# A message-passing layer on one core: the third update layer in an iteration of its own, first tables made on other engines, and a shorter order for the last blocks

## The chip, the core and the metric

The kernel runs on one core of a Trainium2 chip. Its time is the device time of one execution in microseconds. Engines are TensorE (PE, with its weight loads PEld), VectorE (DVE), ScalarE (ACT), GpSimd (POOL) and SyncE (SP, which issues DMAs). They run each their own list of instructions in order and wait for each other on semaphores.

## The reference

128 graphs of 64 nodes with 128 features. For each edge (i, j) of a graph a three-layer network (layer norm after the first two) gives a message; the messages of a node are summed, and a second such network updates the node:

```python
messages = _mlp(concat[f_i, f_j], msg_w0 ... msg_b2)
messages = messages * coupling_matrix[..., None]
agg = jnp.sum(messages, axis=2)
updated = part_feats + _mlp(concat[part_feats, agg], upd_w0 ... upd_b2)

def _mlp(x, w0, b0, g0, be0, w1, b1, g1, be1, w2, b2):
    h = _layernorm(jax.nn.relu(x @ w0 + b0), g0, be0)
    h = _layernorm(jax.nn.relu(h @ w1 + b1), g1, be1)
    return h @ w2 + b2
```

Some one in eight pairs has an edge, so the kernel computes messages only for listed edges.

## The kernel before, in words

**Edges.** Two graphs form a pair; each graph has 640 edge slots in 5 tiles of 128. A *chunk* is 4 tiles, a *quarter* 5 chunks (two pairs), a *block* 4 pairs (10 chunks). There are 160 chunks, 32 quarters and 16 blocks.

**The loop.** `edge_path` writes the program out as numbered iterations `n`. In each, PE does layer 1 of chunk n-8 (`layer1`, L546, bank `z`), layer 0 of chunk n (`layer0`, L499, bank `hps`), transposes `h` of chunk n-1 (`stats0`, L510, bank `hT`) and makes the selection marks of chunk n+2 (`marks`, L486, bank `mk`). DVE takes the statistics of `hT` (L518), compares `mk` with the table `cmpt` into `s` (L497) and takes the statistics of `y` (L564). ACT turns `hps` into `h` (L508) and `z` into `y` (L557). Beside this, each iteration has places ("a", "m", "b", "x", "x1", "x2", "e1", "e", run in the order at L905 to L922) to which a dictionary `plan` assigns functions by iteration number through `at(n, place, ...)`. An engine's order of work is the order in which this loop issues. So what stands at "a" goes first on ACT, what stands at "m" first on DVE, and what stands at "x" last on PE.

**Quarters.** `var0_of`, `root_of`, `turn_root` make the standard deviation of layer 0 (`m_sd`, `sh`, `sdT`), `var1_step`, `root1_of`, `inverse_of` the inverse one of layer 1 (`m_v`, `m_sq`, `m_q`). `node_marks` and `weights` (L625) make per-node weights `w`, and `reduce` (L637) sums messages per node into bank `ys`.

**The update of a block** is a `Unit`, a chain over 14 iterations: `sums_out` (`ysum`), a transpose (`turn`, `turn_out`), first layer from `xn` and `ysum` (`u0a`, `w2u`) with `layer_out` into `uh`, its statistics and root, a transpose, second layer (`u1c`) into `uy`, statistics and root, a transpose, third layer (`u2c`), and `finish` (L734), which writes `uo` and sends it out. `bias0` (L672) makes the additive part `m0` of the first layer, `residual` the one of the last. The last block is cut into two units of half its width.

**Banks.** All three layers of a unit, `rows` (the first-layer products of a block's nodes, L443) and the products of derived weights share the one bank `mu` (`ubank`, L316, one buffer); transposes share two banks `ma`.

**The start.** Constants and derived matrices are made while the first blocks run: `derivation` (L175) lists 13 products through `mu`, one per iteration, with scaled weights and broadcasts made on POOL (L181, L207) and the banks emptied by DVE (L190, L201). `bias_table` and `bias_part` (L569, L595) make the table `b1t` that layer 1 needs, the latter on ACT in 20 operations.

Of the kernel before, what the change touches and what calls it, by code (L numbers as in the profile page):

```python
# [23 lines left out]
def tile_gnn(  # L24
# [79 lines left out]
    def load_first(b, q0, q1):  # L104
# [37 lines left out]
    nc.vector.memset(lt, 1.0)  # L142
    nc.gpsimd.affine_select(out=lt, in_=lt, pattern=[[1, P]], compare_op=ALU.is_ge,
                            fill=0.0, base=0, channel_multiplier=-1)
    first = const.tile([P, PB, N], F32, name="first")
# [3 lines left out]
    make_identity(nc, ident)  # L149

# [11 lines left out]
    nc.vector.memset(lt[0:N, N:P], 0.0)  # L162

    slot = const.tile([P, CAP], F16, name="slot")
    nc.gpsimd.iota(slot, pattern=[[1, CAP]], base=0, channel_multiplier=0,
                   allow_small_or_imprecise_dtypes=True)
    cmpt = const.tile([P, 4 * CAP], F16, name="cmpt")
    nc.vector.memset(cmpt[0:N, 0:CAP], 1.0)
# [123 lines left out]
    def edge_path(es):  # L292
# [23 lines left out]
        def ubank():  # L316

            return ps_u.tile([P, 512], F32, name="mu")

# [275 lines left out]
        def bias_part(c):  # L595
            for t in range(CH * c, CH * c + CH):
                nc.scalar.activation(W["b1t"][:, t, :], W["b1mix"], AF.Copy,
                                     scale=W["tile_of"][:, t:t + 1])
# [26 lines left out]
        def weights(p):  # L625
# [3 lines left out]
            for g in range(2):  # L629
                k = (2 * h + g) * TG  # L630
                (nc.vector if p == NP - 2 else nc.gpsimd).tensor_tensor(  # L631
# [21 lines left out]
        class Unit:  # L653


            def __init__(self, b, k0, n, eng):
                self.b, self.k0, self.n, self.eng = b, k0, n, eng
                self.s = slice(k0 * P, (k0 + n) * P)
                self.q = slice(k0, k0 + n)
                self.blk = blocks[b]  # L660

        def wide(name, u):
            t = updp.tile([P, PB, C], F32, name=name)
            return t[:, 0:u.n, :]
# [24 lines left out]
        def turn_out(u, src):  # L689
            t = updp.tile([P, PB * P], F32, name=src + "T")  # L690
            setattr(u, src + "T", t)
            nc.scalar.copy(t[:, 0:u.n * P], u.ps[:, 0:u.n * P])

        def layer(u, *pairs):
            ps = ubank()
# [9 lines left out]
        def layer_out(u, o, bias):  # L705
# [3 lines left out]
            st = updp.tile([P, PB, 6], F32, name=o + "_st")[:, 0:u.n, :]  # L709
# [4 lines left out]
        def upd_m0(u):  # L714
            u.m2 = square_sum(updp, u.st, u.n, f"um0_{u.n}", u.eng)

        def upd_root0(u):
            u.sd = root0(updp, u.m2, u.n, f"um0_{u.n}")
# [6 lines left out]
        def upd_m1(u):  # L725
            u.v1 = var1_of(updp, u.st, u.m2, u.n, f"um1_{u.n}", u.eng)

        def upd_root1(u):
            u.v1 = root1(updp, u.v1, u.n, f"um1_{u.n}")

        def upd_inverse(u):
            u.q1 = inverse(updp, u.v1, u.n, f"um1_{u.n}")
# [15 lines left out]
        SC = QC + L1 + QC  # L748
        for b in range(NB):
# [23 lines left out]
            if b < NB - 1:  # L773
                units = [(Unit(b, 0, PB, nc.gpsimd), o + QC + SC)]
# [3 lines left out]
            for u, n in units:  # L778
                at(n + 1, "a", sums_out, u)
                at(n + 1, "e", bias0, u)  # L780
                at(n + 2, "x", turn, u, "ysum")
                at(n + 3, "a", turn_out, u, "ysum")
                at(n + 3, "x", lambda u: layer(u, ("xn", u0a), ("ysumT", W["w2u"])), u)
                at(n + 4, "m", layer_out, u, "uh", "m0")
                at(n + 4, "e", upd_m0, u)
                at(n + 6, "a", upd_root0, u)
                at(n + 6, "e", upd_shift, u)
                at(n + 7, "x", turn, u, "uh")
                at(n + 8, "a", turn_out, u, "uh")
                at(n + 8, "x", lambda u: layer(u, ("uhT", W["u1c"])), u)  # L790
                at(n + 8, "e", residual, u)
                at(n + 9, "m", layer_out, u, "uy", "usdb")
                at(n + 9, "e", upd_m1, u)
                at(n + 11, "a", upd_root1, u)
                at(n + 11, "m", upd_inverse, u)
                at(n + 12, "x", turn, u, "uy")
                at(n + 13, "a", turn_out, u, "uy")
                at(n + 13, "x", lambda u: layer(u, ("uyT", W["u2c"])), u)
                at(n + 14, "m", finish, u)
        for p in range(NP):  # L800
# [4 lines left out]
            at(w, "x", node_marks, p)  # L805
            at(w + 1, "a", node_marks_out, p)
            at(w + 2, "e1", weights, p)
            at(p // 2 * QC + SC, "x1", reduce, p)
# [280 lines left out]
```

## Time and profile before

| | us |
|---|---|
| median of 3 runs (lowest, highest) | 700.18 (699.29, 700.63) |
| profiled execution, its time | 698.02 |
| profiled execution, span from first to last instruction | 696.3 |
| PE busy | 636.4 (91%) |
| DVE busy | 503.2 (72%) |
| ACT busy | 359.0 (52%) |
| POOL busy | 361.8 (52%) |
| mean granted TensorE clock | 0.961 |

In the profile's rows, "L701 PE MATMUL mu<-u0a,xnT" is an instruction of line 701 on PE that reads `u0a` and `xnT` and writes `mu`; a bracket behind a row is the engine's idle time before it and what ended that. An fp32 matmul has two records. A busy share of PE is not its share of peak. PEclk is the granted clock, 1.00 being full.

### The profile page before, as it was taken

The numbers are of one execution on the slowest core, as the hardware profiler recorded it, in microseconds if no ns is written. First come the engines' busy times: TensorE is split into PE (matmuls) and PEld (weight loads), VectorE is DVE, ScalarE is ACT, GpSimd is POOL, SyncE is SP. The second block draws the span as 40 slices with busy tenths as digits, with TensorE's granted clock in tenths as the row PEclk, the third lists the DMA queues.
The fourth block names the chain that finished last, engine by engine and source line by source line (L and its number), as shares of the span: only waits on it lengthen the run. The fifth ranks groups of instructions, "written<-read, shape, count | busy, mean of one in ns | idle before, by whom it ended". The sixth has DMA issues, their size and how long they took to land.

```text
span 696.3 us, 15879 instructions
## 1 busy us (share of the span) xinstructions
PE 636.4 (91%) x5873; PEld 584.2 (84%) x5873; DVE 503.2 (72%) x1917; ACT 359.0 (52%) x814; POOL 361.8 (52%) x932
## 2 busy tenths in 40 slices
PE   6799999899998989989898998989899898989874
PEld 5688899798898979889897998989799898978762
DVE  6788778778587867858786785877768586776453
ACT  3655565555454546536454663645556364554330
POOL 7443555548274554827455382745638364453550
PEclk8999999999999999999999999999999999999986
DMA  5000000100101010010101001010000000000001
GB/s 130 16 24 1 9 2 1 40 2 1 39 2 39 2 39 1 2 39 1 39 2 39 2 1 39 3 39 2 7 25 2 16 2 16 1 2 16 16 2 32
DMA packets 27916, 12.06 MB, mean 17 GB/s; under 512 B 10422, under 2 KB 27836, under 8 KB 27836
## 3 DMA queue, kind: packets, MB, share of 16 engines
q1 hardware_dynamic: 27548, 10.89, 5.8%
q8 instruction: 47, 0.77, 0.5%
q14 instruction: 33, 0.27, 0.1%
q10 hardware_dynamic: 288, 0.13, 0.1%
HBM read 6.82 MB, written 4.19 MB: 16 GB/s over the span
## 4 chain that ended last, share of the span: by engine, by line


## 5 line engine op out<-in xcount | busy, mean ns | idle before, releaser
L518 DVE BATCH_NORM_STATS2 st<-hT 128x6 f32<-128x128 f32 x640 | 141.8, 283 | 69.6 <-PE hT L514 64.1
L554 PEld LDWEIGHTS z<-w1c,h 128*128 128x128 f32 x1280 | 168.4, 192 | 7.1
L554 PE MATMUL z<-w1c,h 128*128 128x128 f32 x1280 | 168.8, 274 | 0.0
L631 POOL TENSOR_TENSOR w<-oh,m_q 128x320 f32<-128x320 f16 x126 | 88.8, 726 | 114.2 <-PE hT L514 100.4
L564 DVE BATCH_NORM_STATS2 st<-y 128x6 f32<-128x128 f32 x640 | 137.5, 275 | 7.2 <-ACT y L557 7.2
L557 ACT ACTIVATE y<-z 128x512 f32<-128x512 f32 x160 | 95.9, 599 | 89.5 <-PE z L554 87.4
L508 ACT ACTIVATE h<-hps,b0c 128x512 f32<-128x512 f32 x160 | 109.3, 683 | 5.2 <-PE hps L505 5.2
L497 DVE TENSOR_TENSOR s<-mk,cmpt 128x512 fp32r<-128x512 f32 x160 | 107.4, 671 | 0.1
L514 PE MATMUL hT<-ident,h 128*128 128x128 f32 x640 | 97.4, 275 | 0.0
L505 PE MATMUL hps<-s,abl 128*128 128x512 f32 (+3 forms) x256 | 92.1, 371 | 2.8 <-ACT h L508 2.8
L514 PEld LDWEIGHTS hT<-ident,h 128*128 128x128 f32 x640 | 76.5, 141 | 9.7
L551 PE MATMUL z<-b1t,sdT 80*128 80x512 f32 x160 | 78.8, 492 | 1.1 <-ACT y L557 1.1
L505 PE MATMUL hps<-s,abh 128*128 128x512 f32 (+3 forms) x256 | 78.3, 324 | 0.0
L646 PE MATMUL ys<-y,w 128*64 128x128 f32 x1280 | 77.8, 277 | 0.0
L646 PEld LDWEIGHTS ys<-y,w 128*64 128x64 f32 x1280 | 70.1, 138 | 3.4 <-issue 0.2
L701 PE MATMUL mu<-u0a,xnT 128*128 128x128 f32 x128 | 34.8, 365 | 34.1 <-DVE uo L737 32.6
L490 PE MATMUL mk<-tp,qs 128*128 128x512 f16 (+3 forms) x256 | 61.4, 301 | 3.4 <-DVE s L497 2.8
L701 PEld LDWEIGHTS mu<-u0a,xnT 128*128 128x128 f32 x128 | 26.9, 259 | 37.3 <-DVE uo L737 35.3
L465 DVE TENSOR_TENSOR abl<-mu,abh 128x512 fp32r<-128x512 f32 x32 | 22.1, 690 | 49.0 <-ACT abh L458 49.0
L505 PEld LDWEIGHTS hps<-s,abl 128*128 128x128 f32 x256 | 49.5, 193 | 3.5 <-ACT h L508 3.2
L252 POOL TENSOR_TENSOR um_d<-uh_st 128x4 f32<-128x4 f32 x15 | 3.1, 207 | 92.6 <-DVE uh_st L711 92.6
L622 ACT CAST oh<-ma 128x384 f16<-128x384 f32 (+1 forms) x128 | 48.5, 433 | 3.5 <-PE ma L615 0.5
(209 smaller groups left out, 1104.5 us busy)
## 6 DMA issues: line engine op xcount, KB each, us to landing
xn<-in_x_dram SPq DMA_DIRECT2D x15, 256.0 KB, 3.2
out_dram<-uo SPq DMA_DIRECT2D x15, 256.0 KB, 2.4
an<-in_adj_dram SPq DMA_DIRECT2D x16, 128.0 KB, 3.0
xn<-in_x_dram SPq DMA_DIRECT2D x2, 128.0 KB
out_dram<-uo SPq DMA_DIRECT2D x2, 128.0 KB, 2.1
w<-in_L_gnn_msg_w_dram SPq DMA_DIRECT2D x2, 64.0 KB, 2.9
u<-in_L_gnn_upd_w_dram SPq DMA_DIRECT2D x2, 64.0 KB, 2.0
w0a<-in_L_gnn_msg_w_dram ACTq DMA_DIRECT2D x1, 64.0 KB, 2.1
```

The lines of the kernel that those rows point to most:

```text
L497: nc.vector.tensor_tensor(S[n], MK.pop(n), cmpt[:, o:o + CH * P], op=ALU.is_equal)
L505: nc.tensor.matmul(ps[:, c:c + w], lhsT=ab[:, g % 4, :], rhs=s[:, c:c + w], start=(k == 0), stop=(k == 1))
L508: nc.scalar.activation(H[n], ps, AF.Relu, bias=b0c)
L514: nc.tensor.transpose(ps[:, t, :], H[n][:, t * P:(t + 1) * P], ident)
L518: nc.vector.bn_stats(ST0[q][:, CH * c + t, :], ps[:, t, :])
L551: nc.tensor.matmul(ps, lhsT=SD[q], rhs=W["b1t"][:, CH * c:CH * c + CH, :], start=True, stop=False, skip_group_check=True)
L554: nc.tensor.matmul(ps[:, t, :], lhsT=h[:, t * P:(t + 1) * P], rhs=W["w1c"], start=False, stop=True, skip_group_check=True)
L557: nc.scalar.activation(Y[n], ps, AF.Relu)
L564: nc.vector.bn_stats(ST1[q][:, CH * c + t, :], Y[n][:, t, :])
L631: (nc.vector if p == NP - 2 else nc.gpsimd).tensor_tensor(w[:, :, g, :], OH[p][:, :, g, :], Q[q][:, k:k + TG].unsqueeze(2).to_broadcast([P ...
L646: nc.tensor.matmul(YS[b][g * N:(g + 1) * N, k, :], lhsT=w[:, t, g, :], rhs=y, start=(t == 0), stop=(t == TG - 1))
L701: nc.tensor.matmul(ps[:, s], lhsT=l, rhs=w, start=(n == 0), stop=(n == len(pairs) - 1))
```

## The change

Five parts:

1. *Order of a unit.* The fixed offsets become lists. In `STEADY` the third layer moves from offset 13 to 14 and `finish` from 14 to 15; before, offset 13 of one block and offset 3 of the next were the same iteration, and both use `mu`. `bias0` moves from offset 1 to -2.
2. *Last blocks.* `LAST` gives block 14 and the two half units of block 15 shorter lists; the second half unit starts 3 iterations earlier. The half units use the banks of `hps` and `z` (`hbank`, `zbank`), whose own work is over by then. The last quarter's marks are made two iterations earlier, its weights all on DVE, its root one iteration earlier. The first half unit's small statistics go from DVE to POOL.
3. *Tables at the start.* The constant memsets and `iota`s for `lt`, `cmpt`, `slot` and one element of `dq` go to POOL or ahead; `cmpt`'s second memset (1920 columns on DVE between two compares) becomes 960 columns on DVE at the very start and 1600 on POOL. The step table of block 0 comes from two matmuls into two banks, emptied by ACT and DVE at once.
4. *Derived matrices.* Scalings and broadcasts go from POOL to ACT, right ahead of their product; plain products are emptied by ACT instead of DVE. `bias_part` goes from ACT (4 operations a chunk) to POOL (one a chunk).
5. *Buffers.* A unit's tiles are one per block and shared by its half units; `uo` and the statistics have two buffers.

The core of the diff:

```diff
-            nc.gpsimd.tensor_scalar(wg, w, g, None, op0=ALU.mult)
             def product():
+                nc.scalar.activation(wg, w, AF.Copy, scale=g)
...
-                nc.vector.tensor_copy(W[name], ps[:, :C])
+                nc.scalar.copy(W[name], ps[:, :C])
...
-            nc.gpsimd.tensor_copy(beb, be.to_broadcast([P, P]))
             def fn(ps):
+                nc.scalar.copy(beb, be.to_broadcast([P, P]))
...
+        def hbank():
+            return ps_h.tile([P, CH * P], F32, name="hps")
+        def zbank():
+            return ps_z.tile([P, CH, C], F32, name="z").rearrange("p t c -> p (t c)")
...
         def bias_part(c):
-            for t in range(CH * c, CH * c + CH):
-                nc.scalar.activation(W["b1t"][:, t, :], W["b1mix"], AF.Copy,
-                                     scale=W["tile_of"][:, t:t + 1])
+            t = slice(CH * c, CH * c + CH)
+            nc.gpsimd.tensor_tensor(W["b1t"][:, t, :],
+                                    W["b1mix"].unsqueeze(1).to_broadcast([4 * QT, CH, C]),
+                                    W["tile_of"][:, t].unsqueeze(2).to_broadcast([4 * QT, CH, C]),
+                                    op=ALU.mult)
...
-                (nc.vector if p == NP - 2 else nc.gpsimd).tensor_tensor(
+                (nc.vector if p // 2 == NQ - 1 else nc.gpsimd).tensor_tensor(
...
         def layer(u, *pairs):
-            ps = ubank()
+            ps = u.bank()
...
+        STEADY = (1, 2, 3, 3, 4, 7, 8, 6, 8, 9, 12, 13, 11, 14, 15)
+        LAST = ((1, 2, 3, 3, 4, 4, 5, 6, 5, 7, 7, 8, 9, 8, 9),
+                (1, 1, 2, 2, 3, 3, 4, 4, 4, 5, 5, 6, 7, 6, 7),
+                (1, 2, 3, 3, 4, 4, 5, 5, 5, 6, 6, 7, 7, 7, 8))
...
-                units = [(Unit(b, 0, 2, nc.vector), o + SC), (Unit(b, 2, 2, nc.vector),
-                                                              o + QC + SC)]
+                units = [(Unit(b, 0, 2, nc.gpsimd, hbank), o + SC, LAST[1]),
+                         (Unit(b, 2, 2, nc.vector, zbank), o + QC + SC - 3, LAST[2])]
...
-                at(n + 1, "e", bias0, u)
+                at(n - 2, "e", bias0, u)
...
-                at(n + 13, "a", turn_out, u, "uy")
-                at(n + 13, "x", lambda u: layer(u, ("uyT", W["u2c"])), u)
-                at(n + 14, "m", finish, u)
+                at(n + t[11], "a", turn_out, u, "uy")
+                at(n + t[12], "a", upd_root1, u)
+                at(n + t[12], "m", upd_inverse, u)
+                at(n + t[13], "x", lambda u: layer(u, ("uyT", W["u2c"])), u)
+                at(n + t[14], "m", finish, u)
...
+            last = p // 2 == NQ - 1
+            m = w - 2 if last else w
+            at(m, "x", node_marks, p)
+            at(m + 1, "a", node_marks_out, p)
+            at(NCHK + L1 + 1 if last else w + 2, "e1", weights, p)
+            at(NCHK + L1 + 2 if last else p // 2 * QC + SC, "x1", reduce, p)
...
+        nc.gpsimd.memset(cmpt[0:N, 3 * CAP // 2:4 * CAP], 1.0)
...
+        for g in range(2):
+            ps = (abank, zbank)[g]()
+            nc.tensor.matmul(ps[:, 0:PB * N], lhsT=dq,
+                             rhs=blocks[0]["pos"].rearrange("p q j -> p (q j)"), start=True,
+                             stop=True)
...
-        nc.vector.memset(cmpt[0:N, CAP:4 * CAP], 1.0)
...
         for c in range(QC):
-            at(4 + c, "a", bias_part, c)
+            at(4 + c, "e", bias_part, c)
```

How the rows of the engines' lists move is shown at three places. First PE in the steady part, from the marks of the iteration in which a block's first update layer runs. Before (`u2c` is the third layer of the block ahead, `u0a` and `w2u` the first layer of this one):

```order
L490 MATMUL mk<-tp,qs 128x128
L701 MATMUL mu<-u2c,uyT 128x128 x4
L701 MATMUL mu<-u0a,xnT 128x128
L701 MATMUL mu<-w2u,ysumT 128x128
...
L421 MATMUL ma<-pos,dq 128x256
L538 MATMUL ma<-ident,sh 80x128
L551 MATMUL z<-b1t,sdT 128x512
L554 MATMUL z<-w1c,h 128x128 x4
```

and now, with the iteration behind it:

```order
L498 MATMUL mk<-tp,qs 128x128
L715 MATMUL mu<-u0a,xnT 128x128
L715 MATMUL mu<-w2u,ysumT 128x128
...
L429 MATMUL ma<-pos,dq 128x256
L546 MATMUL ma<-ident,sh 80x128
L559 MATMUL z<-b1t,sdT 128x512
L562 MATMUL z<-w1c,h 128x128 x4
...
L498 MATMUL mk<-tp,qs 128x512
L715 MATMUL mu<-u2c,uyT 128x128 x4
L443 MATMUL ma<-ident,xn 128x128 x4
```

`u2c` has moved from the place right ahead of `u0a` to the end of the next iteration.

Second POOL in the steady part, at the two operations of `bias0` (`c2u,deg` and `ub0b`). Before they stand behind the last operation of `var1_step` (`m_v`) and ahead of the next quarter's weights `w`:

```order
L255 TENSOR_SCALAR m_d<-m_d 128x20
L256 TENSOR_TENSOR m_4624<-m_d,m_s 128x20
L270 TENSOR_TENSOR m_v<-m_v,m_4624 128x20
L674 TENSOR_TENSOR m_4682<-c2u,deg 128x512
L677 TENSOR_TENSOR m_4682<-m_4682,ub0b 128x512
L631 TENSOR_TENSOR w<-oh,m_q 128x5x64 x2
```

and now behind `residual` (`xo`) of the block ahead, some 15 operations earlier:

```order
L541 TENSOR_TENSOR sh<-m_sd,sh 128x40
L641 TENSOR_TENSOR w<-oh,m_q 128x5x64 x2
L695 TENSOR_TENSOR xo<-xn,cu2b 128x512
L688 TENSOR_TENSOR m_4472<-c2u,deg 128x512
L691 TENSOR_TENSOR m_4472<-m_4472,ub0b 128x512
L270 TENSOR_SCALAR um_v<-um_4212 128x4
```

`bias0` has moved ahead of the unit's second variance (`um_v`), of the next block's edge table and of `var1_step`.

Third ACT in the first iterations, where `h` is the output of layer 0 and `b1t` the bias table. Before:

```order
L508 ACTIVATE h<-hps,b0c 128x512 x2
L585 CAST b1hi<-b1b 128x128
L458 CAST abh<-mu 128x512
L597 ACTIVATE b1t<-b1mix,tile_of 80x128 x4
L508 ACTIVATE h<-hps,b0c 128x512
```

and now, with a broadcast (`b1b_b`), an emptied product (`b1b`) and a scaling (`w2c_g`) that were on POOL and DVE:

```order
L516 ACTIVATE h<-hps,b0c 128x512
L211 COPY b1b_b<-be0c 128x128
L203 COPY b1b<-mu 128x128
L516 ACTIVATE h<-hps,b0c 128x512
L593 CAST b1hi<-b1b 128x128
L466 CAST abh<-mu 128x512
L516 ACTIVATE h<-hps,b0c 128x512
L185 ACTIVATE w2c_g<-w_79,g1c 128x128
```

The four `b1t` operations ahead of an `h` are gone from ACT, and short copies stand behind each `h` instead.

More of the change, by code (lines that the diff above doesn't have):

```diff
@@ L149, in tile_gnn @@
     make_identity(nc, ident)
+    cmpt = const.tile([P, 4 * CAP], F16, name="cmpt")
+    nc.gpsimd.iota(cmpt[N:P, :], pattern=[[0, 4], [1, CAP]], base=1, channel_multiplier=0,
+                   allow_small_or_imprecise_dtypes=True)
+    nc.vector.memset(cmpt[0:N, 0:3 * CAP // 2], 1.0)
+    slot = const.tile([P, CAP], F16, name="slot")
+    nc.gpsimd.iota(slot, pattern=[[1, CAP]], base=0, channel_multiplier=0,
+                   allow_small_or_imprecise_dtypes=True)
     dq = const.tile([P, P], F32, name="dq")
@@ L660, in __init__ @@
                 self.blk = blocks[b]
+                self.tag = "" if n == PB else f"_{k0}"
         def wide(name, u):
-            t = updp.tile([P, PB, C], F32, name=name)
-            return t[:, 0:u.n, :]
+            if name not in u.blk:
+                u.blk[name] = updp.tile([P, PB, C], F32, name=name,
+                                        bufs=2 if name == "uo" else 1)
+            return u.blk[name][:, u.q, :]
         def sums_out(u):
@@ L708, in layer_out @@
             setattr(u, o, t)
[L709 removed]
+            st = updp.tile([P, PB, 6], F32, name=o + "_st", bufs=2)[:, 0:u.n, :]
             for q in range(u.n):
@@ L830, in edge_path @@
         count_out(0)
+        nc.gpsimd.memset(dq[N:N + 1, N - 1:N], 0.0)
         marks_table(0)
-        nc.gpsimd.iota(cmpt[N:P, :], pattern=[[0, 4], [1, CAP]], base=1, channel_multiplier=0,
-                       allow_small_or_imprecise_dtypes=True)
+        nc.gpsimd.memset(cmpt[0:N, 3 * CAP // 2:4 * CAP], 1.0)
         turn_x(0, 0, 2)
@@ L836, in edge_path @@
         place_first()
-        nc.vector.memset(dq[N:N + 1, N - 1:N], 0.0)
         for p in range(2):
```

87 lines of the change are left out of this document (39 added, 48 removed).

## Prediction

> **What bounds the kernel now.** I read the waits of TensorE first, because PE is the busiest engine of the page. The five longest groups, as engine, line and tile, what is waited for, then us in total, times and the longest:
>
> ```profile
> PE mu L701 <- DVE uo L737: 34.8, 16, 2.6
> PE mu L701 <- ACT uyT L692: 3.6, 2, 2.1
> PE ma L538 <- POOL sh L533: 3.2, 4, 1.1
> PE hps L505 <- ACT h L508: 2.8, 2, 2.5
> PE mk L490 <- DVE s L497: 2.8, 2, 1.9
> ```
>
> One wait is ten times the next: matmuls into the bank `mu` wait for the last step of the update, `uo`. Where it sits shows the timeline, once for PE and once for DVE (start, length, operation, and in brackets the idle time before it):
>
> ```profile
> 171.80 1.11 PE L701 MATMUL mu<-u2c,uyT 128*128 128x128 f32 x8
> 175.28 0.80 PE L701 MATMUL mu<-u0a,xnT 128*128 128x128 f32 x2 [2.37 <-DVE uo L737]
> ```
>
> ```profile
> 173.34 0.85 DVE L564 BATCH_NORM_STATS2 st<-y 128x6 f32<-128x128 f32 x4
> 174.12 1.10 DVE L737 SCALAR_TENSOR_TENSOR uo<-mu,um_q,xo 128x128 f32<-128x128 f32 x4
> 178.88 0.69 DVE L245 CUSTOM_DVE_ANT_0 uh<-mu,m 128x512 f32<-128x512 f32 x1 [3.66 <-PE mu L701]
> ```
>
> In one iteration PE computes the third layer of block b-1 (`u2c`) and then the first of block b (`u0a`) into the same single bank. DVE reaches `uo` only behind the statistics of that iteration, so PE stands 2.37 us; then DVE stands 3.66 us for PE. To see how often this happens and what else it costs, I cut the steady part into windows from one such `u0a` to the next, 13 of them (length; busy us and instructions of PE, PEld, DVE, ACT, POOL; granted clock; DMA):
>
> ```profile
> 95.70:135.40 39.70, 37.41 (x366) 34.77 (x364) 33.02 (x126) 22.95 (x52) 24.12 (x61) 1.00 0.01 2
> 135.50:175.20 39.70, 37.41 (x364) 34.78 (x364) 30.29 (x115) 21.86 (x49) 22.25 (x58) 1.00 0.07 18
> 175.30:216.50 41.20, 38.85 (x364) 36.23 (x364) 30.31 (x115) 21.86 (x49) 22.25 (x58) 0.96 0.07 18
> 216.50:256.30 39.80, 37.47 (x364) 34.85 (x364) 30.32 (x115) 21.86 (x49) 22.27 (x58) 1.00 0.07 18
> ...
> sum 530.10, PE 499.40 PEld 464.75 DVE 395.81 ACT 285.05 POOL 287.21; mean PE 38.42 PEld 35.75 DVE 30.45 ACT 21.93 POOL 22.09
> ```
>
> Every window holds the same 364 matmuls. Apart from the one gap, PE is busy from end to end: 39.80 less 37.47 leaves 2.33 us, the stall. Windows come in two lengths: where the mean clock reads 0.96 the same work takes 1.4 us more. Cut finer, the clock after the stall at 172.9 reads
>
> ```profile
> 174.00:175.20 1.20, 0.00 (x0) 0.00 (x0) 1.20 (x6) 0.00 (x0) 0.00 (x0) 0.86 0.00 0
> 175.20:176.00 0.80, 0.72 (x3) 0.72 (x4) 0.02 (x1) 0.00 (x0) 0.00 (x0) 0.50 0.00 0
> ```
>
> so in some blocks the stall is followed by a few us at half clock. The kernel is thus bound by PE, with a periodic stall that sometimes takes the clock with it. DVE with 30.45 us of a mean window of 40.8 is next.
>
> **The stall (steady part).** The change puts `u2c` one iteration later, behind `u0a`, and `uo` too. `u0a` then finds `mu` free, since what stood there before, `rows`, was read two iterations earlier; it follows at once. What is late next? `u2c` now needs `uh` read out of `mu`. In the old trace DVE was through the iteration's statistics at 174.2, so `uh` would take until about 174.9 (0.69); PE goes on from 171.8 with four pairs of `u0a` and `w2u` (16 records, twice the 8 of `u2c`, which take some 0.9: 1.7) and the next iteration's own matmuls (about 3, since ten iterations with all their layers take 37.45), and so is at `u2c` near 176.5. Spare: about 1.5 us. And `rows` of the iteration after that needs `uo`, 1.10 us of DVE at that iteration's start, while PE has layers and a whole `reduce` ahead of `rows`. No wait of the kind is left, so a block takes PE's own 37.45 us at full clock (the rows with 1.00): 13 x 37.45 = 486.9, and 530.1 - 486.9 = **43.2 us saved**: 30.8 of gaps (13 x 2.37) and 12.4 of low clock. DVE's 30.45 us fit in 37.45.
>
> [...]
>
> `bias0`, two POOL operations, moves from one iteration behind a pass to two ahead of it, in front of `var1_step` of the next quarter. Their prices, the operations around them, and what ACT and PE do with the result:
>
> ```profile
> 246.78 0.23 POOL L270 TENSOR_TENSOR m_v<-m_v,m 128x20 f32<-128x20 f32 x1
> 246.96 1.04 POOL L674 TENSOR_TENSOR m<-c2u,deg 128x512 f32<-128x512 f32 x1
> 248.08 1.28 POOL L677 TENSOR_TENSOR m<-m,ub0b 128x512 f32<-128x512 f32 x1
> ```
>
> ```profile
> 248.07 0.32 ACT L276 ACTIVATE m_sq<-m_v,eps_c 128x20 f32<-128x20 f32 x1
> 248.72 0.60 ACT L557 ACTIVATE y<-z 128x512 f32<-128x512 f32 x1 [0.33 <-PE z L554]
> ```
>
> ```profile
> 250.44 0.48 PE L551 MATMUL z<-b1t,sdT 80*128 80x512 f32 x1
> ```
>
> `m_v` is ready 2.3 us later, near 249.3, and `m_sq` runs near 249.35; `y` queues behind it on ACT, from 248.72 to 249.7, and ends at 250.3. PE needs that bank at 250.44: still in time, by 0.15 us. I take nothing for it; without that margin it costs up to 1 us a block.
>
> **The start.** Four places matter (DVE, ACT, then PE):
>
> ```profile
> 9.64 1.66 DVE L849 MEMSET cmpt<- 64x1920 f16 x1 [0.34 <-issue]
> ...
> 11.40 0.69 DVE L497 TENSOR_TENSOR s<-mk,cmpt 128x512 fp32r<-128x512 f32 x1
> ```
>
> ```profile
> 20.26 0.29 ACT L585 CAST b1hi<-b1b 128x128 fp32r<-128x128 f32 x1
> ...
> 23.94 1.28 ACT L597 ACTIVATE b1t<-b1mix,tile_of 80x128 fp32r<-80x128 f32 x4 [1.96 <-POOL b1mix L591]
> 25.12 0.67 ACT L508 ACTIVATE h<-hps,b0c 128x512 f32<-128x512 f32 x1
> ```
>
> ```profile
> 12.15 0.58 PE L490 MATMUL mk<-tp,qs 128*128 128x256 f16 x2 [1.90 <-DVE s L497]
> ...
> 25.85 0.50 PE L505 MATMUL hps<-s,abl 128*128 128x512 f32 x1 [2.54 <-ACT h L508]
> ```
>
> The memset of 1.66 us between two compares goes to POOL, so the compare comes 1.66 sooner; the second `dq` matmul and its copy take back some 0.3, leaving 1.3. The five groups of 1.28 us in `b1t` leave ACT, and with them the 2.54 us that PE waited for `h`. Against this ACT gets 17 small copies (four scalings, four broadcasts, nine bank copies), about 0.29 each by the `b1hi` row, 4.9 us in 20 iterations. The nine copies hide in ACT's idle time. The eight others stand behind `h` on ACT and directly ahead of a matmul: 0.67 + 0.29 after `hps`, against 0.5 to 0.8 of PE work; four of the eight have other PE work in front, so 4 x 0.35 = 1.4 lost. Sum 1.3 + 2.5 - 1.4 = **2.4 us saved**. The ends: -2 (each of the eight waits 0.7) and +4.4 (both idle times, 1.90 + 2.54, nothing lost).
>
> **The end.** PE's and DVE's lines of the last 40 us:
>
> ```profile
> 657.38 0.49 PE L701 MATMUL mu<-u0a,xnT 128*128 128x128 f32 x2 [1.73 <-DVE uo L737]
> ...
> 671.32 3.30 PE L646 MATMUL ys<-y,w 128*64 128x128 f32 x40
> ...
> 678.58 0.68 PE L701 MATMUL mu<-u1c,uhT 128*128 128x128 f32 x4 [1.36 <-DVE uo L737]
> ...
> 686.85 1.20 PE L701 MATMUL mu<-u1c,uhT 128*128 128x128 f32 x4 [0.85 <-DVE uo L737]
> ```
>
> ```profile
> 681.99 0.42 DVE L245 CUSTOM_DVE_ANT_0 uh<-mu,m 128x256 f32<-128x256 f32 x1 [1.65 <-PE mu L701]
> ...
> 692.13 0.61 DVE L737 SCALAR_TENSOR_TENSOR uo<-mu,um_q,xo 128x128 f32<-128x128 f32 x2 [1.43 <-PEq L1052]
> ```
>
> A 14th stall, 1.7 us, goes like the others. After the last `reduce` (ends 674.62) the last half block needs 7.4 us to `uh` and 10.75 more to the end of `uo`, since three passes share `mu` and step in turns. With own banks the waits for `uo` (1.36 and 0.85) fall away, and the transposes go ahead of the roots on ACT. Walking the new order by hand with these durations, I get about 5.3 us to `uh` and 7.5 from it, so 5.3 saved. The last `reduce` starts 3.5 us after its weights, behind a second and a first layer; now only a transpose and half a first layer stand there: 1.5 saved. Sum 1.7 + 5.3 + 1.5 = **8.5 us**; the ends are 4 (the waits for `uo` and the 14th stall alone) and 12 (each half pass at its own durations).
>
> The last weights move from two engines to one:
>
> ```profile
> 665.85 1.65 POOL L631 TENSOR_TENSOR w<-oh,m_q 128x320 f32<-128x320 f16 x2 [0.61 <-DVE m_q L281]
> 665.90 1.94 DVE L631 TENSOR_TENSOR w<-oh,m_q 128x320 f32<-128x320 f16 x2
> ```
>
> Four on DVE cost 3.9 us by this row, or 1.9 to 2.0 if each takes half of it with POOL at rest; in the new order POOL has nothing to do there, so I take no loss, with 2 us as the end. [...]
>
> **Sum.** 43.2 + 2.4 + 8.5 = 54.1. The profiled execution took 698.02 (span 696.3 and 1.72 around it): 643.9. The median of the runs, 700.18, lies 2.16 above it; with this added, **646**.
>
> **Rivals.** *The wait moves* (0.11). Some in-order queue is late where the stall was: `y` behind `m_sq` behind POOL, or `u2c` behind `uh`. For it: a margin of only 0.15 us at 250.44, and DVE and POOL lose the 4 us in which they caught up. Against it: DVE itself waits 3.66 us after each stall. Price: about 1 us x 14 blocks, 660. *The clock dips stay* (0.07): half clock comes of its own, as the mean 0.96 of some windows but not of others could mean. Against it: the finer windows put the dip into the gap. Price 12.4: 658. [...] *The clock falls under unbroken load* (0.03), the slower side: nothing pauses PE any more, and the granted clock drops for good. The place is the steady part from the first missing stall on; 487 us of PE work at clock c take 487/c, and the 54 us are gone at c = 0.90; at 0.85 it is 732. Against it: windows of 37 us without a pause read 1.00. [...]
>
> **How the numbers follow.** The forecast has 0.78. With start (4.4) and end (12) at their best it is 640.5, and 638 if the 2.16 between profile and median does not return; with start (-2), end (4), weights (2) and 2 us in the steady part all at their worst it is 659, and as these hardly meet I take 655. The two cheaper rivals reach 660 and are taken in: 638 to 661. What is left out is the slower case and the corners. A difference of 0.2%, 1.4 us, is about what this measurement can tell from none. Faster 0.96 (forecast, both cheap rivals), same 0.01, slower 0.03.
>
> **What would show it.** Right: windows of one block near 37.5 us with clock 1.00, no wait for `uo` in PE's list in the steady part, PE's idle before 30 us below 4, the last `uo` less than 8 us behind its `uh`. Wrong: a new line on top of PE's waits, `uh` or `y` as releaser; blocks of 38.5 or more; clock 0.96 without a gap.

## The result and the profile after

| | before | changed |
|---|---|---|
| median of the runs | 699.73 us (697.32 to 700.63, 4 runs) | 643.06 us (640.71 to 645.9, 4 runs) |
| span of the profiled run | 696.3 us | 639.0 us |
| mean granted clock | 0.961 | 0.993 |

The ratio is 0.9197, with a 95% interval of 0.9152 to 0.9241: 56.7 us less, where 54 were forecast (646 us; range 638 to 661).

The waits of TensorE in the changed kernel (waiting operation and what released it; us in total, times, longest):

```profile
PE ma L701 <- DVE uy L247: 4.2, 3, 2.6
PE ma L546 <- POOL sh L541: 4.0, 4, 1.5
PE mu L921 <- DVE uo L751: 2.3, 1, 2.3
PE mk L498 <- DVE s L505: 1.7, 2, 1.3
...
PE mu L187 <- ACT u2c_g L185: 0.4, 1, 0.4
PE mu L187 <- ACT u1c_g L185: 0.4, 1, 0.4
PE mu L187 <- ACT w2c_g L185: 0.4, 1, 0.4
PE mu L715 <- DVE uo L751: 0.3, 1, 0.3
```

The line of 34.8 us is down to 0.3. Two lines stand out: a turn of `uy` in the last blocks (2.6 us at once), and one wait for `uo` by line 921, which is no layer but the flag's small matmul. The steady part, cut as in the prediction from one first layer to the next (length; busy us and instructions of PE, PEld, DVE, ACT, POOL; granted clock; DMA), and below it nearly the whole of it in one window:

```profile
134.25:171.45 37.20, 37.20 (x365) 34.81 (x364) 30.09 (x116) 21.94 (x50) 22.55 (x59) 1.00 0.07 19
171.45:208.65 37.20, 37.20 (x365) 34.81 (x364) 30.09 (x116) 21.93 (x50) 22.55 (x59) 1.00 0.07 19
...
36.00:580.00 544.00, 541.41 (x5250) 504.17 (x5249) 437.65 (x1678) 320.36 (x717) 317.91 (x823) 1.00 0.06 15
```

A block takes 37.20 us, all of it PE busy, at clock 1.00. At the place of the old stall, on PE, the third layer now stands behind the first and one iteration's matmuls:

```profile
205.63 0.39 PE L715 MATMUL mu<-w2u,ysumT 128*128 128x128 f32 x2
...
208.65 1.05 PE L715 MATMUL mu<-u2c,uyT 128*128 128x128 f32 x8
```

And DVE's answer there:

```profile
206.37 0.67 DVE L247 CUSTOM_DVE_ANT_0 uh<-mu,m 128x512 f32<-128x512 f32 x1
...
210.81 1.11 DVE L751 SCALAR_TENSOR_TENSOR uo<-mu,um_q,xo 128x128 f32<-128x128 f32 x4
```

No brackets: neither engine waits. `uh` is through at 207.04, `u2c` starts at 208.65, so 1.6 us are spare.

Where the 57.3 us of span went: the first `u0a` starts at 93.30 instead of 95.69 (2.4 us); from there to the first `u0a` of block 13 it is 482.6 us instead of 530.5 (47.9); from there to the end 63.1 instead of 70.2 (7.1). The middle stretch needs a correction: with `u2c` behind the next `u0a`, it holds one third layer less than before (its first block takes 36.31 us instead of 37.20), and the last stretch one more. For like work it is about 47.0 in the middle and 8.0 at the end.

### The profile page after: what moved, and what is told of

Read it like the earlier page. It is cut to its first block, busy times and chain, and to the rows that moved or that the text cites. A ratio compares the mean times of both kernels' runs of the same rounds, so it can differ in the third digit from the quotient of the medians.

```text
span 639.0 us, 15850 instructions
## 1 busy us (share of the span) xinstructions
PE 615.1 (96%) x5875; PEld 567.0 (89%) x5875; DVE 497.6 (78%) x1894; ACT 358.6 (56%) x811; POOL 368.4 (58%) x943
## 4 chain that ended last, share of the span: by engine, by line
## 5 line engine op out<-in xcount | busy, mean ns | idle before, releaser
L641 POOL TENSOR_TENSOR w<-oh,m_q 128x320 f32<-128x320 f16 x124 | 86.9, 722 | 127.4 <-PE hT L522 110.9
L466 ACT CAST abh<-mu 128x512 fp32r<-128x512 f32 x32 | 18.7, 585 | 54.8 <-PE mu L459 54.8
L513 PEld LDWEIGHTS hps<-s,abh 128*128 128x128 f32 x256 | 49.1, 192 | 0.0
L559 PEld LDWEIGHTS z<-b1t,sdT 80*128 80x128 f32 x160 | 30.3, 190 | 8.9 <-issue 3.1
```

Of the source, the lines that this page charges most:

```text
L513: nc.tensor.matmul(ps[:, c:c + w], lhsT=ab[:, g % 4, :], rhs=s[:, c:c + w], start=(k == 0), stop=(k == 1))
L559: nc.tensor.matmul(ps, lhsT=SD[q], rhs=W["b1t"][:, CH * c:CH * c + CH, :], start=True, stop=False, skip_group_check=True)
L641: (nc.vector if p // 2 == NQ - 1 else nc.gpsimd).tensor_tensor(w[:, :, g, :], OH[p][:, :, g, :], Q[q][:, k:k + TG].unsqueeze(2).to_broadca ...
```

## The experiments

The theory to be tested: the gain is the stall of the next block's first layer in bank `mu` and the half clock behind it; head and tail are small. The rivals: the clock dips have their own cause; or the gain comes from the head, the tail or the moved POOL work.

**The shift alone.** On the kernel before:

```
-                at(n + 13, "x", lambda u: layer(u, ("uyT", W["u2c"])), u)
-                at(n + 14, "m", finish, u)
+                at(n + 13 + (u.n == PB), "x", lambda u: layer(u, ("uyT", W["u2c"])), u)
+                at(n + 14 + (u.n == PB), "m", finish, u)
```

> The kernel before with one edit: in whole blocks the third update layer and its finish one iteration later; head, tables and last blocks as they were. Theory (gap and half clock both belong to the wait of the next block's first layer for uo, and go with it): 13 blocks at about 37.2 us instead of 40.8, clock 1.00, less the 14th stall (1.7), plus one stall of 2.3 that the flag's matmul meets: about 654 us. Rival, the clock dips are not the gap's: only 13 x 2.37 + 1.7 - 2.3 = 30 go, about 669, with windows of mean clock 0.96 left. Rival, the gain is in the head and the tail: 690 or more.

Measured: 650.2 us, ratio 0.9277 (0.9243 to 0.9312), 50.5 us less than before in the same comparison. Both rivals fall; the 654 expected was 4 us too high. In its trace the stretch from the first `u0a` to that of block 13 takes 482.8 us at full clock, against 482.6 in the changed kernel, so that stretch owes its gain to the shift.

**The shift undone.** On the changed kernel:

```
-        STEADY = (1, 2, 3, 3, 4, 7, 8, 6, 8, 9, 12, 13, 11, 14, 15)
+        STEADY = (1, 2, 3, 3, 4, 7, 8, 6, 8, 9, 12, 13, 11, 13, 14)
```

> The changed kernel with the third layer of the whole blocks before block 14 back in its old iteration; everything else as changed. Theory: 13 stalls of 2.37 and the half clock behind most of them come back, the flag's stall of 2.3 goes: 643 + 46 - 2 = about 687 us. Rival, dips are not the gap's: 643 + 30.8 - 2.3 = 672. Rival, the old place costs nothing any more because bias0 and the tables are elsewhere: 643.

Measured: 693.32 us, ratio 0.9885 (0.9845 to 0.9924), 50.3 us slower than the changed kernel. The 687 expected was 6 us too low: 46 had been put for the steady part, and its trace has 49.7 (532.3 instead of 482.6), with nine of the first twelve stalls followed by half clock instead of eight. The wait is back as the top line:

```profile
PE mu L715 <- DVE uo L751: 33.0, 14, 2.4
```

From both sides the shift is worth 50 us; that leaves 0.9885, some 8 us (5 to 11), for head and tail together.

**The gap filled.** On the kernel before, behind the third layer of whole blocks, extra matmuls whose result nobody reads:

```
+        def fill():
+            ps = abank()
+            for q in range(11):
+                nc.tensor.matmul(ps[:, 0:P], lhsT=mean_m, rhs=mean_m, start=True, stop=True)
...
+                    at(n + 13, "x", fill)
```

> The kernel before, with 11 matmuls of 128x128 on constants (2.4 us at full clock) behind the third layer of each whole block, into a bank of their own; the next first layer still waits for uo. They are extra work that fills the stall. Theory (half clock comes from PE standing still for 2.37 us): the clock stays at 1.00 and the 12.4 us of low clock go, 687 us. Rival, the dips have another cause: 700 us, and up to 2 more where the fill is longer than the gap. If the fill only costs: 699.7 + 13 x 2.4 = 731.

Measured: 685.35 us, ratio 0.9787 (0.9761 to 0.9813). More work in the same place is 15.4 us faster. Its third layer, the fill, the first layer behind it, and one window:

```profile
213.53 1.11 PE L706 MATMUL mu<-u2c,uyT 128*128 128x128 f32 x8
214.48 2.62 PE L682 MATMUL ma<-mean_m 128*128 128x128 f32 x22
217.01 0.49 PE L706 MATMUL mu<-u0a,xnT 128*128 128x128 f32 x2
```

```profile
175.30:215.10 39.80, 39.80 (x388) 37.27 (x387) 30.29 (x117) 21.86 (x49) 22.17 (x59) 1.00 0.07 18
```

The first layer still comes at the old distance behind `u2c`, but no block falls below clock 1.00. So in these blocks half clock came from PE standing still. It was worth 12.5 us in the stretch of the 13 blocks (518.0 instead of 530.5 in the traces); by the medians the edit gains 15.4 in all.

**The gap doubled.** On the kernel before, ahead of the real finish of whole blocks, its four operations twice more into a scratch tile:

```
+                d = updp.tile([P, PB, C], F32, name="again")
+                for r in range(2):
+                    for q in range(u.n):
+                        nc.vector.scalar_tensor_tensor(d[:, q, :], u.l_ps[:, q, :],
+                                                       u.q1[:, q:q + 1], u.xo[:, q, :],
+                                                       op0=ALU.mult, op1=ALU.add)
```

> The kernel before, with the four finishing operations of each whole block on DVE done twice more into a scratch tile ahead of the real ones (8 x 0.275 = 2.2 us), so that the gap in PE is about 4.6 us. Theory (the longer PE stands, the surer the half clock): 13 x 2.2 = 29 us of gap and half clock behind all 13 gaps instead of 8, another 5 x 1.55 = 8: about 737 us. Rival, dips are independent of the gap: 729. If DVE had to catch up and waits spread: over 745.

Measured: 750.47 us, ratio 1.0729 (1.0698 to 1.0759): 50 us slower, neither the 737 nor the 729 of the first two. The gaps are 4.4 us, near the 4.6 meant, so 2.07 x 13 = 27. The stretch of the 13 blocks grew by 41.6 us (572.1 instead of 530.5), so about 15 more are clock: PE is busy at half clock for 58 us of it instead of 26. Another 9.5 came behind this stretch (79.7 us to the end instead of 70.2), where block 14's gap is doubled too (3.79 instead of 1.73) and half clock lasts longer. One gap:

```profile
225.25 0.79 PE L701 MATMUL mu<-u0a,xnT 128*128 128x128 f32 x2 [4.44 <-DVE uo L744]
```

and the granted clock (the last figures but two) around that gap, in pieces of 3.41 us:

```profile
220.02:223.43 3.41, 0.79 (x8) 0.60 (x6) 3.41 (x15) 0.29 (x1) 1.41 (x3) 1.00 0.00 0
223.43:226.84 3.41, 1.59 (x7) 1.59 (x8) 1.77 (x7) 0.00 (x0) 0.00 (x0) 0.50 0.19 57
226.84:230.26 3.42, 3.42 (x15) 3.06 (x14) 1.06 (x3) 0.34 (x1) 0.00 (x0) 0.50 0.52 135
230.26:233.67 3.41, 3.41 (x30) 3.24 (x29) 1.88 (x8) 2.54 (x8) 1.20 (x6) 1.00 0.01 2
```

Half clock lasts 6.83 us here, twice 3.41, and so in 11 of the 13 blocks. Measured to 0.1 us, each of the 8 dips in the 13 blocks of the kernel before lasts 3.41 us, and all start at whole multiples of 3.413 us from one another (24, 36, 60, 72, 84, 108 and 120 of them behind the first). The clock thus changed at the borders of fixed windows of 3.413 us. Two stalls of the kernel before, of equal length, cut by that grid, first the window that holds most of the stall, then the next:

```profile
335.29:338.70 3.41, 1.57 (x14) 1.30 (x12) 3.41 (x14) 1.04 (x4) 1.63 (x3) 1.00 0.00 0
338.70:342.11 3.41, 2.88 (x22) 2.71 (x23) 1.16 (x3) 0.35 (x1) 0.00 (x0) 1.00 0.56 152
```

```profile
376.25:379.66 3.41, 1.04 (x10) 0.85 (x9) 2.76 (x11) 0.00 (x0) 1.07 (x2) 1.00 0.00 0
379.66:383.07 3.41, 3.41 (x18) 3.08 (x16) 0.59 (x1) 0.00 (x0) 0.00 (x0) 0.50 0.71 195
383.07:386.48 3.41, 3.41 (x29) 3.24 (x28) 2.07 (x10) 2.62 (x6) 1.20 (x6) 1.00 0.02 4
```

The first stall lies across a border, PE stands still for 1.85 us of the window (busy 1.57), and the clock stays. The second lies within one window, 2.37 us (busy 1.04), and the next window runs at half clock: 18 instructions in it instead of 29. Of 24 stalls laid on the grid (the first 12 of the kernel before and of the kernel with the shift undone) all with 1.95 us or more in one window are followed by half clock, 17 cases, and none with 1.85 or less, 7 cases. The two 13th stalls had 1.91 us, without half clock behind it, and 2.00 us, with it. That gives a forecast.

**The gap shortened.** On the kernel before, third layer and finish of whole blocks moved into a place of their own, `f`, that runs ahead of `stats1`:

```
+                f = u.n == PB
+                at(n + 13, "f" if f else "x", lambda u: layer(u, ("uyT", W["u2c"])), u)
+                at(n + 13 if f else n + 14, "f" if f else "m", finish, u)
...
+            run(n, "f")
             if 0 <= n - L1 < NCHK:
                 stats1(n - L1)
```

> The kernel before, with uo put ahead of the statistics of y in DVE's order of that iteration: the stall in PE stays, but is about 0.85 us shorter (1.5 instead of 2.37). Theory from the dips of the first runs: PE's clock is set in fixed windows of 3.41 us, and a window with 1.95 us or more of standing still is followed by one at half clock (1.71 us of work lost), one with 1.85 or less is not. A gap of 1.5 can't fill that share of any window: no dip in any block, 13 x 0.85 = 11 us of gap and 8 x 1.71 = 13.7 us of clock go, about 676 us. Rival, a gap is followed by half clock the likelier the longer it is, 8/13 x 1.5/2.37 of 13, so 5 dips: 685. Rival, DVE's order makes y's statistics late and the wait moves: 690 or more.

Measured: 678.57 us, ratio 0.9695 (0.9655 to 0.9735). One of its stalls:

```profile
213.27 0.49 PE L701 MATMUL mu<-u0a,xnT 128*128 128x128 f32 x2 [1.60 <-DVE uo L737]
```

All twelve gaps up to 565 us last 1.45 to 1.60 us and none is followed by half clock; chance in proportion to length would have given 5. A 13th, of 1.86 us at 604, is, although 1.91 in the kernel before was not: the border is not sharp. The forecast of 676 was 3 us too low, the rival's 685 is outside what the interval allows (676 to 682). Most of the miss is in its two sizes: a block takes 39.06 us instead of 39.82, so 0.76 less and not 0.85, and of the 22.5 us that the 13 blocks gained 12.6 are left for the clock, not 13.7.

One stall of another kernel is outside this rule. In the kernel with the tables back (further down) the flag's wait leaves PE still for 1.75 us of a window, and half clock follows:

```profile
580.95:584.36 3.41, 1.66 (x13) 1.58 (x14) 1.70 (x8) 0.12 (x1) 1.33 (x6) 1.00 0.24 74
584.36:587.78 3.42, 3.42 (x27) 3.16 (x27) 1.71 (x9) 2.10 (x5) 1.04 (x1) 0.50 0.01 3
```

**The flag later.** On the changed kernel:

```
-        at(NCHK - 3, "x", flag_sum)
+        at(NCHK - 2, "x", flag_sum)
```

> The changed kernel with the flag's small matmul one iteration later, so that it no longer asks for the bank of the third layer of block 12 in the iteration in which that is written. Theory (the one stall of the old kind that is left, 2.3 us near 580, goes and nothing takes its place): 640.6 us, and PE without an idle stretch over 1 us from 36 to 595. Rival, the last blocks' chain on DVE and POOL is what ends late and takes it back: 643.

Measured: 640.06 us, ratio to before 0.9152 (0.9122 to 0.9182), 3.0 us under the changed kernel. The line of 2.3 us is gone, and no wait over 1.2 us is left between 36 and 595 us. The intervals of the two kernels overlap; but the three kernels with the later flag lie at 640.1 to 640.9 (two follow below), and the changed one and three others close to it with the early flag at 643.1 to 644.0.

**The last blocks, first try.** In the changed kernel DVE's variance chain for the last quarter looks like this, with POOL's operations of the same 4 us behind it:

```profile
613.88 0.19 DVE L254 TENSOR_TENSOR m_d<-st 128x20 f32<-128x20 f32 x1
613.98 1.30 DVE L255 TENSOR_TENSOR m_s<-st 128x20 f32<-128x20 f32 x1
615.21 0.63 DVE L256 TENSOR_TENSOR m_d<-m_d 128x20 f32<-128x20 f32 x1
...
616.71 0.96 DVE L272 TENSOR_TENSOR m_v<-m_v,m 128x20 f32<-128x20 f32 x1
```

```profile
613.97 1.27 POOL L695 TENSOR_TENSOR xo<-xn,cu2b 128x512 f32<-128x512 f32 x1 [0.71 <-DVE m_v L270]
615.19 0.61 POOL L688 TENSOR_TENSOR m<-c2u,deg 128x256 f32<-128x256 f32 x1
```

Each slow DVE operation ends with a POOL operation that began beside it: 0.19 us becomes 1.30 beside `xo` of 1.27. The edit moves those POOL steps back and a turn behind the last reduce:

```
+                at(n + 1 if t is LAST[2] else n - 2, "e", bias0, u)
...
+                at(n + t[8] + (3 if t is LAST[0] else 0), "e", residual, u)
...
+                at(n + t[10], "x2" if t is LAST[0] else "x", turn, u, "uy")
```

> The changed kernel with three POOL steps of the last blocks (residual of block 14, bias0 of the last half unit) moved behind the last quarter's variance chain on DVE, and the turn of block 14's uy behind the last reduce. Theory (those POOL operations slowed the chain on DVE from about 0.17 to 0.6 to 1.3 us an operation, and the turn held up reduce on PE): the last four weights some 2 us sooner, the last reduce 2.7 us sooner, 640.4 us. Rival, uy of block 14 or the um chain on POOL is late next and takes it back: gain under 1 us, 642.5.

Measured: 644.0 us, ratio 0.9193 (0.9162 to 0.9224): no gain. The chain on DVE is through at 615.93 instead of 617.67, and the last reduce starts at 619.88 instead of 622.40, 2.5 us sooner where 2.7 were forecast. Two things keep it from the end. The weights, forecast 2 us sooner, are not (618.66, before 618.51), since the square root stands on ACT behind a copy that waits for a reduce:

```profile
617.64 0.37 ACT L682 COPY ysum<-ys 128x256 f32<-128x256 f32 x1 [3.28 <-PE ys L656]
617.90 0.31 ACT L278 ACTIVATE m_sq<-m_v,eps_c 128x20 f32<-128x20 f32 x1
```

and `bias0`, now in front of the first half unit's `usdb` on POOL, made its `uy` late; the turn of that waits for it on PE, with the second half's first layer queued behind:

```profile
628.04 0.44 PE L701 MATMUL ma<-ident,uy 128*128 128x128 f32 x2 [1.67 <-DVE uy L247]
```

**Both.** The flag and the last blocks' three lines together.

> Both edits of the two kernels before together. Theory: the gains add, 643.1 - 2.4 - 2.7 = 638 us. Rival, one of them hides behind the other: 640.5.

Measured: 640.85 us, ratio 0.9141 (0.9114 to 0.9169). The 638 expected is missed; it is the same as the flag alone, as the first try's zero would have it.

**The last blocks, second try.** With the later flag; `m0` and `xo` in two buffers:

```
-                (1, 2, 3, 3, 4, 4, 5, 5, 5, 6, 6, 7, 7, 7, 8))
+                (0, 0, 1, 1, 2, 2, 3, 3, 3, 4, 4, 5, 5, 5, 6))
...
+                at(n - 2 if t not in LAST[1:] else NCHK, "e", bias0, u)
...
+                at(n + (2 if t is LAST[0] else t[8]), "e", residual, u)
...
+            at(n + L1 + (0 if q == NQ - 1 else 2), "e" if q == NQ - 1 else "a", root1_of, q)
```

> The kernel with the later flag, and for the last blocks: residual of block 14 and both bias0 of block 15 early (two buffers each), the last quarter's square root on ACT ahead of the copy out of ys, the turn of block 14's uy behind the last reduce, and the second half unit one to two iterations sooner, ahead of the first half's second layer. Theory (in the first try the root sat behind that copy in ACT's order, bias0 in front of the first half's usdb on POOL, and the second half's turn behind the first half's waits on PE): the last reduce starts 2.5 us sooner and the last uo ends under 10 us behind it: 640.1 - 3.5 = about 636.5 us. Rival, the halves now collide on DVE and POOL and take it back: 640.

Measured: 640.86 us, ratio 0.9162 (0.9135 to 0.919): the rival's 640. The root now comes at once (0.04 us behind its chain, which runs at 0.17 to 0.20 an operation), and the last reduce starts 5.8 us behind the end of block 13's `uo` instead of 8.5. But from the reduce's end to the last `uo` it is 11.8 us instead of 10.6: the second half's `uy` waits 2.04 us for a `usdb` that stands on POOL behind the first half's chain. The rest was lost earlier, by the edit itself: both `bias0` of block 15 now run on POOL from 591.64 to 594.45, beside DVE's operations for the last quarter's first root (`m_d` to `m`), which take 2.1 us instead of the 0.8 in the kernel with the later flag alone. PE's wait for that root's `sh` grows from 0.90 to 2.19 us, and 6.83 us of half clock follow:

```profile
594.87 0.31 PE L546 MATMUL ma<-ident,sh 128*80 128x128 f32 x1 [2.19 <-POOL sh L541]
```

From block 13's first `u0a` to block 14's it is 33.19 us instead of 29.51, and from there to the end 30.2 instead of 32.7: 3.7 lost, 2.6 won.

**The tail undone.** On the changed kernel, the last two blocks with the old offsets and banks (and the last marks, weights, root and reduce at their old places):

```
+        LAST = (STEADY, STEADY[:13] + (13, 14), STEADY[:13] + (13, 14))
...
+                units = [(Unit(b, 0, 2, nc.vector, ubank), o + SC, LAST[1]),
+                         (Unit(b, 2, 2, nc.vector, ubank), o + QC + SC, LAST[2])]
```

> The changed kernel with the last two blocks as before: block 14 in the steady order, the last block's halves by the old offsets, both in bank mu, last weights, reduce and marks at their old places. The third layer of the whole blocks stays one iteration later. Theory (the end was worth 8.5, of it 1.7 for a stall that stays away here): 643.1 + 6.8 = about 650 us. Rival, the end was hardly worth anything, since DVE's chain for the last quarter is now slowed beside POOL: 645 or less.

Measured: 646.46 us, ratio 0.9236 (0.9201 to 0.9271): between the 650 expected and the rival's 645. By the medians the new tail is worth 3.4 us, half of the 6.8 expected; the intervals of the two kernels just overlap.

**The derived matrices' tables back.** On the changed kernel:

```
+            nc.gpsimd.tensor_scalar(wg, w, g, None, op0=ALU.mult)
...
-                nc.scalar.activation(wg, w, AF.Copy, scale=g)
...
-                nc.scalar.copy(W[name], ps[:, :C])
+                nc.vector.tensor_copy(W[name], ps[:, :C])
...
+            nc.gpsimd.tensor_copy(beb, be.to_broadcast([P, P]))
...
-                nc.scalar.copy(beb, be.to_broadcast([P, P]))
```

> The changed kernel with the scaling and the broadcast for the derived matrices back on POOL at the start and the copies out of the bank back on DVE; b1t stays on POOL. Theory (on ACT they wait behind h, and each of four products holds PE up for 0.4 us): the four waits go, 643.1 - 1.4 = 641.7 us. Rival, the twelve operations in front of POOL's queue make the first tables late: 643 or more, with a longer wait of PE before 30 us.

Measured: 643.2 us, ratio 0.9191 (0.9156 to 0.9226): no difference; the 641.7 expected is missed. The four short waits go, and one comes back in their place: PE waits for `abl` on DVE, which stands behind an operation that had waited 1.81 us for POOL. The rival had forecast the time, and POOL as its cause.

```profile
21.94 0.46 PE L187 MATMUL mu<-w2c_g,mean_m 128*128 128x128 f32 x2 [1.68 <-DVE abl L473]
```

In this trace the first `u0a` comes at 92.59, earlier than in any with the changed head (93.08 to 95.43), so a small gain is not excluded; two half-clock windows later in this run, which the profiled run of the changed kernel lacks, would hide it.

**bias0 back.** On the changed kernel:

```
-                at(n - 2, "e", bias0, u)
+                at(n + 1 if t is STEADY else n - 2, "e", bias0, u)
```

> The changed kernel with bias0 of the whole blocks before block 14 back behind the reduce on POOL (n + 1 instead of n - 2); all else as changed. Theory (the move cost nothing, its place on POOL hid behind a margin of 0.15 us in front of y): 643.1 us, within 0.2%. Rival, the early bias0 makes the quarter's root and y late by part of its 2.3 us once a block: up to 1 us a block, so 630 to 640. Rival, back at its old place it makes the first layer's uh wait: over 645, with uh waiting for POOL.

Measured: 643.42 us, ratio 0.9178 (0.9155 to 0.9202): the move is worth nothing either way.

## Why the prediction was right, point by point

**The stall: right in its mechanism, low by 4.** Forecast 43.2, measured 47.9 by the spans of 13 blocks, of which 0.9 is the third layer that moved out of this stretch: 47.0. The term that was mis-sized is the gap. The block was put at 37.45 us, PE's busy time in the old windows; it is 37.20, since the old busy time held another 0.25 a block that belongs to the stall: before, two first layers at full clock lie 39.82 us apart (so in the kernel with the filled gap, in nearly every block), 2.62 above 37.20, not the 2.37 in the bracket. That makes 13 x 2.62 = 34.1 where 30.8 were forecast. The low clock, put at 12.4, was 12.5 (530.5 to 518.0 with the gap filled). Together 46.6; 0.4 is left. Half of 3.41 us for each of the 8 dips would be 13.7, more than measured: blocks with a dip took 1.42 to 1.69 us longer. The spare of `u2c` behind `uh`, forecast 1.5, is 1.6. A slip without weight: the first window of the prediction's table has 366 records, not the 364 said of every one.

**"No wait of the kind is left": wrong once.** The flag's matmul asks for `mu` in the very iteration into which the change puts a `u2c`, and waited 2.3 us; before, it stood elsewhere than a third layer. The later flag took 3.0 us off.

**The clock rivals: settled.** *The dips stay* is refuted by the filled gap, where they go though the kernel has its old order. A gap did not have to fill a window of 3.413 us for it: 1.95 us within one was enough each time. *The clock falls under unbroken load* did not happen: 1.00 over 544 us.

**`bias0`: cost 0, right, for a partly wrong reason.** In the block read for it, it ran at 227.17 to 229.57, with six us of other POOL work between it and the next quarter's variance chain, not directly ahead of that chain; the chain ended at 237.54, `y` behind it at 238.37, and PE's next `z` began at 238.77. The margin is 0.40 us instead of the forecast 0.15. *The wait moves* is refuted: no wait of PE over 1.2 us in the steady part but the flag's.

**The start: 2.4 forecast, 2.4 in the trace pair, 2.7 over all traces.** PE's first large wait fell from 1.90 to 1.35 and the 2.54 for `h` is gone; the wait for `sh` near 27 us grew from 0.94 to 1.49; three products wait 0.4 and one broadcast 0.3, 1.5 together, forecast 1.4. One pair of traces can't carry 2.4, since the first `u0a` moves by some us from run to run. But in five traces with the old head it came at 95.69 to 99.02 (mean 97.0), in eight with the changed head at 93.08 to 95.43 (mean 94.2). A part of that is clock, which the forecast did not have: from 10 us on the old heads show two or three windows of half clock, the new ones one each. The sign "PE's idle before 30 us below 4" was not met: it is 5.65 us (8.63 before).

**The end: the size nearly right, in part by luck, the cause half wrong.** Forecast 8.5. The traces differ by 7.1, or 8.0 for like work, with the flag's new 2.3 in that stretch, so 10.3 without it. This pair is a lucky one: with the same last blocks the kernels with the tables back and with `bias0` back took 66.1 and 66.0 us for this stretch instead of 63.1, with two more half-clock windows. And the new tail by itself is worth 3.4. The step that failed is "with own banks the waits for `uo` (1.36 and 0.85) fall away": the first of them falls away without own banks. With the tail undone, PE's lines behind the last `reduce` are

```profile
629.23 0.49 PE L715 MATMUL mu<-u0a,xnT 128*128 128x128 f32 x2 [0.62 <-DVE uy L247]
...
630.91 1.16 PE L715 MATMUL mu<-u2c,uyT 128*128 128x128 f32 x8 [0.52 <-DVE uh L247]
```

The shift puts block 14's third layer too behind the last half's first one, and from the reduce's end (626.3) to the last `uo` (641.0) the old passes take 14.7 us instead of the 18.1 before. Those 3.4 us come with the shift, though a part of them is clock, since the passes before ran longer at half clock; in the kernel with the shift alone the passes took 16.9, much of it at half clock. With the steady part's 47.0 and the 14th stall, less the flag, the shift alone comes to 47.0 + 1.7 + 3.4 - 2.3 = 49.8 at most, and it measured 50.5. The new tail then takes the passes from 14.7 to 10.6: 4.1, of which 3.4 is left in the time. The forecast of 12.8 (5.3 + 7.5) for these passes was 2 us too long: the last `uo` ends 5.7 behind its `uh`. The wait of the last `reduce` behind its weights fell from 3.5 to 2.2, 1.3 of the 1.5 forecast. The last weights cost 1.70 us, as taken: that four on DVE need half of 3.9 us with POOL at rest was the author's estimate, which no trace of the kernel before shows; in the changed kernel POOL has no operation from 617.94 to 621.80, and the four that start on DVE at 618.51 take 1.70 together, where two beside POOL had taken 1.94. Not foreseen was what POOL does beside DVE: the chain of the last quarter takes 3.9 us (613.80 to 617.67) where the second try, with POOL at rest, needs 1.1, and PE waits 2.6 for `uy` behind it. The operation of L255 (`m_s<-st`) takes 1.30 us in this chain, beside POOL's `xo` of 1.27, and 0.20 in the second try. In the first try that of L257 (`m_d<-m_d`) took 1.03 us beside POOL's `usdb` of 1.04, instead of 0.17.

**The sum.** That 646 came within 3 us of 643.06 is in part luck: the steady part gained 4 us more than forecast, and the flag's stall, not seen ahead, took 2.3 back. The 2.16 us added for the distance between profile and median came out as 2.35.

**What stays open.** What decides near the border of the clock rule is not shown, nor why windows in the last blocks follow other figures. Executions of one kernel differ by 1.3 us (gap filled) to 7.2 us (shift alone), the changed one's by 5.2, and windows of half clock in head and tail come and go between them, so gains of one or two us there can't be told by these runs.

## What to carry to other kernels

When two users of a single PSUM bank stand in the same iteration, price the second one's wait as the gap (2.37 us here), plus the slower rows around it (0.25), plus what the clock does after it (12.5 us over 13 gaps). Moving one of them an iteration away cost nothing here where no other user stood in that iteration, so list every user of that bank, also the small ones. In a tail of short operations walk all engines together: what was moved off one queue here landed in front of something on another (waits of 1.67 and 2.04 us). If a gap can't be closed, shortening it (here to 1.6 us), or filling it with matmuls whose result nobody reads, already saved the low clock.

## What the runs showed of the hardware

In the traces the granted clock changed on a fixed grid of 3.413 us that ran on through the program. In the 13 blocks of the steady part, a window at full clock in which PE stood still for 1.95 us or more was followed by a whole window at half clock each time, and one with 1.85 us or less was not; between them both happened (1.91 without, 1.86 with), and the flag's wait just behind these blocks broke the rule once (1.75 us, with). A block with such a window took 1.42 to 1.69 us longer. Nearly equal stalls (2.21 to 2.63 us, most 2.37) were thus dear or cheap by where they fell: dear in 8 of 13.

For the last blocks the border does not hold: in the kernel before, PE stands still for 1.77 us of the window from 662.96 on, in three pauses, and half clock follows.

Windows already at half clock went otherwise: in the kernel with the doubled gap 1.38 to 1.85 us of standing still in them were followed by a second half window, in 11 of 13 blocks. There a block takes 44.2 to 44.6 us for most of the run, near 13 windows (44.37), so that nearly every gap falls alike.
